# Loading an input on ScalarE's DMA queue instead of SyncE's, with eight half strips of it in SBUF instead of five

## The chip, the cores and the metric

The kernel runs on one core of a Trainium2 chip. Five engines work side by side: TensorE (PE in the profile, its weight loads PEld), VectorE (DVE), ScalarE (ACT), GpSimd (POOL) and SyncE (SP). Each takes its own instructions strictly in order and waits on semaphores for the others. A DMA is issued by an instruction on SP, ACT or POOL. That instruction, too, stands in the engine's order: if it has to wait for a buffer, everything behind it on that engine waits with it. The transfer itself is then run by the core's 16 DMA engines, which all queues share.

The metric is device time in microseconds for one launch, the median of several runs.

## The reference

Two layers on a float32 array `x` of 4 images with 512 channels of 64 x 64 points. Layer 0 is a linear attention with two branches; layer 1 an edge detector with a channel attention and a normalisation over the channels. Cut to what is computed:

```python
# layer 0
qkv = concat(h @ wq.T, h @ wk.T, h @ wv.T)             # 512 -> 3 * 512 channels
pw  = grouped_1x1(depthwise_5x5(qkv))                  # second branch
f   = concat(qkv, pw).reshape(B, 128 heads, 24, N)
query, key, value = relu(f[:, :, :8]), relu(f[:, :, 8:16]), f[:, :, 16:]
scores = einsum('bhdn,bhen->bhde', concat(value, 1), key)
out = einsum('bhde,bhen->bhdn', scores, query)
out = out[:, :, :-1] / (out[:, :, -1:] + 1e-15)
x = batchnorm(conv_1x1(out, proj_kernel)) + x
# layer 1
E  = stack(sobel(x), laplace(x), diagonal(x), gradient(x))   # 3x3 filters per channel
ef = concat_k gelu(batchnorm(w_branch[k] @ E[k]))            # 4 branches of 128 channels
ef = ef * sigmoid(w_att2 @ gelu(w_att1 @ mean(ef)))
z  = w_fuse @ ef
result = gelu(layernorm_over_channels(z)) + x
```

## The kernel before

Everything is float32. An image's 4096 points are cut into eight **strips** of 512; a strip of `x` is [128 partitions, 4 channel blocks, 512]. It is loaded as two **half strips** of two channel blocks each, 512 KB a DMA (`load_x`, L260 to L266). Layer 0 runs as sixteen **groups** (class `Group`, L231): four images `b`, and for each the four groups `g` of 128 channels. A group has two phases, each a list of steps made by hand:

- `keys_and_values` (L579 ff.): for every strip in the order `KV_ORDER = (1, 0, 2, ..., 7)` a projection to keys (`project`, L268, 4 matmuls of 128x512) and one to values (`values`, L300, 16 matmuls of 128x128). Between them stand steps of the previous group: the convolution of its queries, its correlations, its divisions.
- `queries`: for every strip in the order `Q_ORDER = (6, 7, 5, ..., 0)` a projection to queries, with the convolution of the keys, the transposes and the first half of the correlations between them.

`project` ends with copies on ACT: `strip` (L283), for queries also `rq` (L281). The strip then goes out by a POOL DMA (L288) and comes back rolled by row (L295).

**Where x stands.** Image 0 loads all its strips once; twelve of its sixteen half strips have a pool of their own (`x_first`), which is closed after group 3. All later images load each strip anew in every phase, except that the last two strips of one phase are kept for the first two of the next (L277, L309). Their half strips are tiles of the pool `xst` with five buffers. A sixth half strip cannot be loaded before one of the five has had its last matmul. This makes 16 loads for image 0 and 100 for each later image, 316 in all. All are issued on SP (L265), which issues nearly all other loads and stores too: `near` (values for the correlations, L318 out and L458 back), `heads` and `cheads` (L405, L575 out, L659, L661 back), `win` (L708), `ef` (L908), `yr` (L890), `out` (L898), `xr` (L674, x once more, for the residual, in a pool of its own) and the weights.

**The stages behind.** While the groups of image b + 1 run, three generators for image b are advanced between the steps of the groups (`run`, `advance`): `project_out` (1x1 convolution, 8 matmuls for each 128 x 512 block), `edge_branches` (filters on DVE and ACT, then branch matmuls) and `fuse_out` (matmuls, normalisation on ACT, DVE and POOL). How far they are advanced is set by shares of time written into the code (`SHARE_Y`, `WAIT_Y`, ...). The last image's stages run alone, after the last group.

**What sets the order.** For PE the order is the program's own (`manual_schedule` with PE, L108). The other engines' orders, DMA issues included, are made when the kernel is built, by a planner that places an instruction where its inputs and its buffer come free by its own reckoning, and prefers what stands earlier in the program. The order is then fixed. Each DMA issued on SP or ACT also takes one of eight counting semaphores in turn, and waits until the DMA that had it before has landed.

Matmul results go to eight PSUM banks: four for single tiles (`ps`), four for sets of four (`quad`). On SBUF, the pools of the groups end at 156,672 bytes of a partition, and the pools of the stages behind begin at 171,872 at the lowest while the groups run. A half strip takes 4,096.

Of the kernel before, what the change touches and what calls it, by code (L numbers as in the profile page):

```python
# [89 lines left out]
def conv_seq_kernel(  # L90
    ctx: ExitStack, tc, x, wqkv, dpk, wtab, proj, projc, pwk, bn0, consts, vec, watt1, batt1, watt2, wbr, wfuse, out
):
    nc = tc.nc
# [5 lines left out]

    front = ctx.enter_context(ExitStack())  # L100
    keep = front.enter_context(tc.tile_pool(name="keep", bufs=1))
    xst = front.enter_context(tc.tile_pool(name="xst", bufs=5))
    mini = front.enter_context(tc.tile_pool(name="mini", bufs=2))
    gw = front.enter_context(tc.tile_pool(name="gw", bufs=2))
    vals = front.enter_context(tc.tile_pool(name="vals", bufs=VALS))
# [125 lines left out]
    class Group:  # L231
# [28 lines left out]
        def load_x(self, j):  # L260
            xs[self.b, j] = []
            for n in range(2):
                pool = x_first if self.b == 0 and j not in Q_ORDER[:2] else xst
                xt = pool.tile([P, 2, 512], F32, name="xt", tag="xt")
                nc.sync.dma_start(out=xt, in_=x[self.b, j, :, 2 * n : 2 * n + 2, :])  # L265
                xs[self.b, j] += [xt[:, 0, :], xt[:, 1, :]]  # L266

        def project(self, t, j):  # L268
# [873 lines left out]
```

## Time and profile before

| | |
|---|---|
| median of 3 runs | 4831.98 us (4826.22 to 4835.85) |
| profiled execution | 4830.43 us, of which the span from first to last instruction is 4828.6 us |
| mean granted clock of TensorE | 0.968 |
| mean DMA rate | 207 GB/s, 998.02 MB in all |
| PE idle | 4828.6 - 4524.3 = 304.3 us |
| loads of x | 316, from 1.2 to 4038.5 us; the 300 of the later images begin at 94.1 us |

The busy time of each engine by stretch of the span, us:

| stretch, us | what runs | PE | DVE | ACT | POOL | DMA share |
|---|---|---|---|---|---|---|
| 0 to 600 | groups of image 0 | 571.04 | 149.06 | 113.25 | 119.65 | 0.68 |
| 600 to 1100 | image 1, projection out of image 0 | 485.89 | 94.52 | 56.68 | 75.23 | 0.76 |
| 1100 to 2000 | images 1 and 2, edges and fusion of image 0 | 847.89 | 473.96 | 389.04 | 203.02 | 0.77 |
| 2000 to 2450 | image 2, projection out of image 1 | 418.10 | 113.71 | 63.46 | 69.77 | 0.73 |
| 2450 to 3300 | images 2 and 3, edges and fusion of image 1 | 785.45 | 438.84 | 353.39 | 194.69 | 0.77 |
| 3300 to 4040 | image 3, projection out and edges of image 2 | 717.47 | 318.66 | 231.90 | 126.78 | 0.75 |
| 4040 to 4828.6 | rest, no load of x by `load_x` | 698.48 | 518.94 | 380.98 | 198.52 | 0.55 |

A line in a view of waits reads: the engine and line that waited, what ended the wait, then the sum in us, the number of times and the longest. `SPq` is SP's queue of DMA issues; its waits cost nothing by themselves, only through what stands behind them. In a timeline, a line gives the start in us, the length in us, the engine, line, operation and tiles, and in brackets the idle time before it and what ended it.

### The profile page before, as it was taken

The page shows a single profiled execution, that of the slowest core. Times are in us where ns is not written, and L with a number is a line of the kernel's source. Part 1 is how long each engine was busy: PE and PEld are TensorE (multiplying, and loading weights), DVE is VectorE, ACT ScalarE, POOL GpSimd, SP SyncE. Part 2 cuts the span into 40 slices and gives each one's busy share as a digit, 9 for nine tenths or more (in the row PEclk, how much of TensorE's full clock was granted, in tenths as well). Part 3 has the DMA queues.
Part 4 walks back from the last instruction along what each step waited for, and adds up shares of the span by engine and source line. Part 5 has one row for each costly group of instructions (what it writes and reads, how often), then busy time and mean ns, then how long its engine had stood idle before and what let it go on. Part 6 is the DMA issues. An engine that isn't in the chain of part 4 may idle for free. (4 is left out here: it accounts for less than half of the span.)

```text
span 4828.6 us, 86405 instructions
## 1 busy us (share of the span) xinstructions
PE 4524.3 (94%) x35900; PEld 2461.5 (51%) x35900; DVE 2107.7 (44%) x2788; ACT 1588.7 (33%) x2719; POOL 987.7 (20%) x1291
## 2 busy tenths in 40 slices
PE   8999999998999999989899999988999999799987
PEld 5554554444566554444465655444446565344433
DVE  1222222114666634311356663441116666447966
ACT  2122121002554523300245452430014545214765
POOL 2111111111121224311111121431111211111443
PEclk9999999999999999999999999999999999899998
DMA  8666679667787877777678778758668887665445
GB/s 228 186 182 183 184 239 259 176 168 192 231 240 230 260 227 220 227 198 188 175 226 255 227 250 231 226 176 223 177 184 233 243 227 227 184 168 151 155 138 172
DMA packets 498327, 998.02 MB, mean 207 GB/s; under 512 B 189160, under 2 KB 221960, under 8 KB 479504
## 3 DMA queue, kind: packets, MB, share of 16 engines
q1 hardware_dynamic: 415760, 722.43, 50.6%
q0 software_dynamic: 82176, 270.07, 20.3%
q8 instruction: 283, 4.64, 0.4%
q14 instruction: 108, 0.88, 0.1%
HBM read 710.67 MB, written 281.61 MB: 206 GB/s over the span
## 5 line engine op out<-in xcount | busy, mean ns | idle before, releaser
L274 PE MATMUL proj<-xt,w_sb 128*128 128x512 f32 x2048 | 953.0, 608 | 50.3 <-DMA xt<-in_x 28.1
L677 PE MATMUL yps<-hd,fold_sb 128*128 128x512 f32 x2048 | 910.5, 600 | 35.8 <-DMA hd<-heads 27.8
L677 PEld LDWEIGHTS yps<-hd,fold_sb 128*128 128x128 f32 x2048 | 386.4, 192 | 531.7 <-issue 466.0
L274 PEld LDWEIGHTS proj<-xt,w_sb 128*128 128x128 f32 x2048 | 380.7, 194 | 541.7 <-issue 453.9
L418 PE MATMUL cv<-rolled,mat 64*32 64x504 f32 (+2 forms) x10240 | 576.4, 598 | 33.1 <-DMA rolled<-flat 19.1
L866 PE MATMUL zps<-ef,wf_sb 128*128 128x512 f32 (+1 forms) x1056 | 469.1, 597 | 45.6 <-DMA ef<-ef 16.7
L305 PEld LDWEIGHTS val<-w_sb,xt 128*128 128x128 f32 x4096 | 472.6, 193 | 43.4 <-issue 29.9
L305 PE MATMUL val<-w_sb,xt 128*128 128x128 f32 x4096 | 487.9, 278 | 2.4 <-DVE vt L312 1.9
L754 PE MATMUL br<-maps,wbr_sb 128*128 128x256 f32 (+1 forms) x1792 | 463.6, 412 | 0.0
L682 DVE SCALAR_TENSOR_TENSOR yt<-yps,shift,xr 128x512 f32<-128x512 f32 x128 | 95.7, 749 | 804.7 <-PE yps L677 757.8
L754 PEld LDWEIGHTS br<-maps,wbr_sb 128*128 128x128 f32 x1792 | 334.8, 189 | 137.4 <-issue 96.4
L288 POOL DMA_DIRECT2D flat<-strip x256 | 144.9, 566 | 1211.9 <-ACT strip L283 1184.8
L418 PEld LDWEIGHTS cv<-rolled,mat 64*32 64x32 f32 x10240 | 196.7, 109 | 381.9 <-issue 355.3
L295 POOL DMA_DIRECT2D rolled<-flat x512 | 273.3, 538 | 558.2 <-PE cv L418 519.5
L283 ACT COPY strip<-proj 128x512 f32<-128x512 f32 x256 | 149.0, 582 | 671.3 <-PE proj L274 671.3
L473 PE MATMUL corr<-near,ckt 128*32 128x160 f32 x8192 | 336.3, 318 | 26.4 <-DMA near<-near 26.2
L866 PEld LDWEIGHTS zps<-ef,wf_sb 128*128 128x128 f32 x1056 | 203.5, 196 | 293.8 <-issue 221.6
L473 PEld LDWEIGHTS corr<-near,ckt 128*32 128x32 f32 x8192 | 261.1, 112 | 122.0 <-issue 68.2
L686 POOL DMA_DIRECT2D y<-yt x128 | 114.4, 894 | 917.1 <-DVE yt L682 756.2
L730 DVE TENSOR_TENSOR maps<-dv 128x1054 f32<-128x1054 f32 (+1 forms) x112 | 159.8, 1427 | 256.8 <-PE br L754 256.7
L897 POOL TENSOR_TENSOR z<-z,yr 128x512 f32<-128x512 f32 (+1 forms) x132 | 175.5, 1348 | 272.7 <-ACT z L894 150.1
L333 ACT ACTIVATE kt<-tr 128x512 f32<-128x512 f32 x128 | 76.2, 595 | 466.4 <-PE tr L331 466.4
(131 smaller groups left out, 4466.0 us busy)
## 6 DMA issues: line engine op xcount, KB each, us to landing
xt<-in_x SPq DMA_DIRECT2D x316, 512.0 KB
near<-near SPq DMA_DIRECT2D x512, 264.0 KB
rolled<-flat POOLq DMA_DIRECT2D x512, 256.0 KB, 7.4
flat<-strip POOLq DMA_DIRECT2D x256, 256.0 KB, 5.8
win<-y SPq DMA_DIRECT2D x96, 396.0 KB
near<-vt SPq DMA_DIRECT2D x512, 66.0 KB
y<-yt POOLq DMA_DIRECT2D x128, 264.0 KB, 6.3
heads<-q SPq DMA_DIRECT2D x128, 256.0 KB
```

The lines of the kernel that those rows point to most:

```text
L274: nc.tensor.matmul(ps, lhsT=self.w[t][:, c, :], rhs=xs[self.b, j][c], start=(c == 0), stop=(c == NCH - 1))
L283: nc.scalar.copy(s, ps)
L288: nc.gpsimd.dma_start(out=self.flat[t][r, :, b : b + 8, :], in_=rows(s))
L295: nc.gpsimd.dma_start(out=self.rolled[t, half][r::8, :, :], in_=self.flat[t][r % 4, :, at : at + 8, :].rearrange("(n c) b w -> c n (b w)", ...
L305: nc.tensor.matmul(ps[:, ts(c, P)], lhsT=xs[self.b, j][n][:, ts(c, P)], rhs=self.w[VALUE][:, n, :], start=(n == 0), stop=(n == NCH - 1),)
L418: nc.tensor.matmul(rows(banks[2 * s + i])[32 * j : 32 * j + 32, :, c0:c1], lhsT=self.mat[t][q, 4 * s + j, (dx + 2) * 4 : (dx + 2) * 4 + 4, :],
L473: nc.tensor.matmul(self.banks[jj][32 * i : 32 * i + 32, 160 * b : 160 * b + 160], lhsT=self.held["c", i][:, at : at + 32], rhs=v[:, 4 * n ...
L677: nc.tensor.matmul(ps, lhsT=fold_sb[g // NG][:, g % NG, ts(c, P)], rhs=hd[g], start=(g == 0), stop=(g == 2 * NG - 1),)
L730: nc.vector.tensor_sub(flat[:, half : 3 * half - 2], dvs[:, 2 : 2 * half], dvs[:, 0 : 2 * half - 2])
L754: nc.tensor.matmul(rows(ps), lhsT=wbr_sb[:, k, c, :], rhs=rows(maps[:, slot[k], c % 2, :], WB)[:, :, 0:W], start=(c == 0), stop=(c == NCH ...
L866: nc.tensor.matmul(ps, lhsT=wf_sb[:, k, ts(c, P)], rhs=ef[k], start=(k == 0), stop=(k == 3))
L897: nc.gpsimd.tensor_add(rows(z), rows(z), rows(yr, WB)[:, :, 1 : W + 1])
```

## The change

Two lines. The pool `xst` gets eight buffers for five, which takes 3 x 4,096 = 12,288 bytes more of a partition. And the load in `load_x` is issued on ACT (`nc.scalar`) for every image but the first (`self.b` is the image's number); image 0 stays on SP.

```diff
-    xst = front.enter_context(tc.tile_pool(name="xst", bufs=5))
+    xst = front.enter_context(tc.tile_pool(name="xst", bufs=8))
...
-                nc.sync.dma_start(out=xt, in_=x[self.b, j, :, 2 * n : 2 * n + 2, :])
+                (nc.scalar if self.b else nc.sync).dma_start(out=xt, in_=x[self.b, j, :, 2 * n : 2 * n + 2, :])
```

So 300 of the 316 issues move from SP's stream into ACT's, among the evictions of PSUM and the activations. The number of loads, their size and the matmuls that read them stay the same, and so does PE's order. The planner lays out the orders of SP, ACT, DVE and POOL anew.

## The prediction

> **What bounds the kernel now.** I read the page first: engine shares and the span in slices.
>
> ```profile
> span 4828.6 us, 86405 instructions
> ...
> PE 4524.3 (94%) x35900; PEld 2461.5 (51%) x35900; DVE 2107.7 (44%) x2788; ACT 1588.7 (33%) x2719; POOL 987.7 (20%) x1291
> ...
> ACT  2122121002554523300245452430014545214765
> ```
>
> PE sets the time: 94% busy, its order fixed. A change that removes no matmul can only touch the 304.3 us in which PE idles (and the clock it is granted after a pause). ACT is busy a third of the time and below 60% in every slice before the last few. The chain that ended last covers only the final 4.2 us, so the question goes to the waits. Those of PE from 94 to 4039 us, the time in which the moved loads are issued:
>
> ```profile
> PE corr L473 <- DMA near<-near: 24.1, 10, 4.8
> PE proj L274 <- DMA xt<-in_x: 22.8, 3, 21.1
> ...
> PE cden L565 <- ACT strip L283: 14.8, 2, 9.8
> PE yps L677 <- DMA hd<-heads: 13.4, 3, 10.5
> PE ctr L445 <- ACT co L431: 11.8, 4, 4.8
> ```
>
> The reader is to see that x costs PE 22.8 us there, nearly all in one wait, and that ACT's lateness costs it too: all lines of this view ended by ACT add up to 44.7 us. Then SP's own waits over the span:
>
> ```profile
> SPq L265 <- PE proj L274: 270.9, 91, 16.3
> SPq L265 <- PE val L305: 225.3, 45, 25.6
> ...
> SPq L458 <- DMA xt<-in_x: 38.4, 33, 3.0
> ```
>
> SP stood 496.2 us before loads of x whose buffer was still being read. That is the wait which the change carries to ACT. The third line shows the other kind: a load of `near` that waits for a load of x to land, because the two share a counting semaphore. Last, the one long wait, in the timelines of SP and PE:
>
> ```profile
> 3228.37 0.33 SPq L265 DMA_DIRECT2D xt<-in_x  x1
> ...
> 3243.57 0.38 SPq L265 DMA_DIRECT2D xt<-in_x  x1
> ...
> 3261.10 0.91 SPq L644 DMA_DIRECT2D fold_sb<-folded  x2
> 3262.05 2.91 SPq L659 DMA_DIRECT2D hd<-heads  x4
> 3265.00 5.49 SPq L661 DMA_DIRECT2D hd<-cheads  x4
> 3270.71 3.97 SPq L318 DMA_DIRECT2D near<-vt  x4
> 3274.86 0.47 SPq L265 DMA_DIRECT2D xt<-in_x  x1
> ```
>
> ```profile
> 3257.47 1.98 PE L274 MATMUL proj<-xt,w_sb 128*128 128x512 f32 x4
> 3280.57 3.70 PE L274 MATMUL proj<-xt,w_sb 128*128 128x512 f32 x4 [21.12 <-DMA xt<-in_x]
> ```
>
> PE has the first half strip and lacks the second, which stands on SP behind the opening burst of `project_out`.
>
> **The change, part by part.**
>
> *Eight buffers, and SP's burst no longer ahead of x.* With three more buffers a load can go when the one three before it went. The load issued at 3274.86 comes third after one at 3122.86 (the same timeline, earlier), so it can go some 120 us sooner, long before the burst. The wait should vanish, and the two short ones with it: 22.8 us. The four pieces after the wait took 3.70 us where the same four took 1.98 before it, since the granted clock averaged 0.82 from 3226 to 3284: 1.7 us more. Together -24.5; the other end is 0, if the load is placed late on ACT for another reason. I take the whole, since two independent causes of the wait are removed at once.
>
> *300 issues on ACT.* No DMA issue on ACT is in the trace. Low end: SP's shortest, 0.327 us, 98 us in all. High end: POOL's for `y`, 0.894 us, 268 us. I take SP's own sum for these 300, 142.0 us, since both engines only start a transfer there. ACT is busy 1207.7 us up to 4040 and idle for 2832, mostly waiting for PE, so this lies in idle time. What gets through I take from ACT's present share: 44.7 us of PE's waits for 1207.7 us of work, 3.7%, so +5.3 us (3.6 to 9.9). Were the cover gone, all 142 would show.
>
> *The waits of these loads, now on ACT.* Behind a waiting load stand evictions of PSUM (`strip`, `rq`, `kt`, `co`), for which PE waits when its four banks of a kind are full, and the edge activations, for which DVE waits. I set each of the 300 issues of the trace beside the next instruction that ACT has after it in the program's order. In 50 cases the issue ended after that instruction had started, 121.0 us in all, the longest 10.1. Only 4.8 us of this is a buffer still being read: the matmuls that free a half strip also release ACT's next work, so ACT would have stood there anyway. 63.2 us (17 cases) is an earlier DMA that had not landed, and the rest is SP busy with its other entries, which ACT does not inherit. So 68.0 us of hold. Low end 3.7% of it, 2.5 us; high end all. The largest case, four loads around 777 to 787 us, holds ACT some 8 us while PE runs a convolution from 780.6 to 789.2 that asks nothing of ACT; the transposes of `co` at 794.7 would start about 1 us late. One part in eight, then: +8.5 us.
>
> *SP without them.* PE's waits for other transfers of SP come to 63.2 us in that window (near 24.1, ef 16.7, hd 13.4 and 3.9, the attention weights 5.1). The 300 issues are 142.0 of SP's 1237.7 us of issuing there, 11.5%, so -7.3 us. High gain: all 63.2. Loss: x now runs beside those transfers instead of behind or ahead of them; 512 KB at the 214 GB/s of that window are 2.4 us, and for 19 such waits that is +46. I stay near zero, since before the longest of them (hd at 2079.8, ef at 3183.8) no load of x stood directly in SP's queue.
>
> The Trainium skill speaks against more here (DMA: Bandwidth & Descriptors, Rules for kernel authors): spreading DMAs over SP, ACT and GpSimd gives no bandwidth, as all run on the same 16 engines; only issue time is saved. By the rule alone the queue term would be those few us and the 24.5 would have to come from the buffers; by the row, where x sat behind the fourteen issues of a burst, order counts as well. The same page (Anatomy of one DMA) puts every semaphore wait on the issuing sequencer, as the waits of SP above show; by that rule alone up to the 68 us would stand on ACT.
>
> *The sum*, against the profiled execution's 4830.4 us, which is 1.6 below the median: 4830.4 - 24.5 + 5.3 + 8.5 - 7.3 = 4812.4, **some 4813 us**. Its own range is 4800 to 4822.
>
> **The rivals.**
>
> *ACT becomes the late engine: slower.* Place: the query phases, where a projection's eviction follows every 3.6 us, and the edge stages, where ACT and DVE hand tiles back and forth. If the new order leaves all 121 us of the lateness counted above on ACT, four tenths of it reaching PE give 4830.4 - 24.5 - 7.3 + 5.3 + 48 = 4852. It decides from 26.5 us on (22%). For it: 44.7 us of PE's waits already end on ACT, and each pause is followed by matmuls at half clock. Against it: the 4.8 us above, and ACT idle two thirds of the time.
>
> *The wait moves on: no change.* The burst at 3261 still has to land, at a DMA share of 0.82 and 249 GB/s; freed of x, PE may wait 20 us later for `hd` or `near` instead, and newly laid out orders of SP and ACT make as many new short waits as they remove. About 4830. For it: 105.1 us of PE's waits in the window end on DMAs, spread over many places. Against it: PE's first use of `hd` after the burst is beyond 3340, and that was no long wait.
>
> *SP was the real trouble: much faster.* Half of the 63.2 us goes: 4830.4 - 24.5 - 31.6 + 13.8 = 4788. Against it: no x directly ahead of the long ones.
>
> **How the numbers follow.** The forecast 0.38, much faster 0.08, no change 0.19, slower on ACT 0.35. A difference under about 0.2%, 9.7 us, could not be told from none. So faster 0.46, within 0.2% 0.19, slower 0.35. The predicted time is that of the forecast. The range takes in no change and most of the slower case, and leaves out the deep ends: 4795 to 4870.
>
> **What would show it.** Right: PE's wait for xt near 3280 is gone, ACT's rows show issues at L265 of 0.3 to 0.5 us, and PE's waits that end on ACT before 4040 grow by less than 15 us. Wrong: issues on ACT near 0.9 us or ACT waiting long on L265 for landings; `strip`, `co` or `ckt` as new first lines of PE's waits; or a wait of the same size on `hd`, `near` or `ef`. The prediction fails as a whole if the newly laid out orders move more than the terms counted here.

## The result and the profile after

The changed kernel took **4882.55 us** (median of 4 runs, 4878.59 to 4892.26) beside 4832.64 us before (4826.22 to 4835.85): a ratio of 1.0108, 95% interval [1.0089, 1.0126]. It is slower by some 50 us, and the time lies above the predicted range. The page first: the span, the shares of the engines, and of the DMA queues SP's (q1) and ACT's (q10), with packets, megabytes and the share of 16 engines' span.

```profile
span 4882.7 us, 86318 instructions
...
PE 4530.8 (93%) x35900; PEld 2465.1 (50%) x35900; DVE 2107.7 (43%) x2788; ACT 1588.5 (33%) x2721; POOL 986.0 (20%) x1291
...
q1 hardware_dynamic: 372560, 565.12, 39.0%
...
q10 hardware_dynamic: 43200, 157.31, 10.7%
```

PE has 6.5 us more of work than before and 47.6 us more of idling. The work of the other engines is the same, and so is that of the DMA engines: all queues together had 71.4% of 4828.6 us before, 3448 us, and have 70.3% of 4882.7 us now, 3433 us. The mean rate fell from 207 to 204 GB/s only because the span grew. So the DMA engines have no more to do than before: something that PE needs comes later. PE's waits from 94 us to 4085 us, just behind the last load of `x` (before: 94 to 4039 us):

```profile
PE corr L473 <- DMA near<-near: 37.1, 9, 13.2
PE cv L418 <- DMA rolled<-flat: 35.0, 6, 9.0
PE over L396 <- DVE rec L381: 19.5, 12, 6.0
...
PE corr L473 <- DMA near<-vt: 16.2, 1, 16.2
...
PE yps L677 <- DMA hd<-cheads: 13.6, 6, 8.8
```

The wait for `xt` is gone from this window altogether. In its place stand `near` (24.1 us before, 53.3 with both its lines), `rolled` (19.1 before) and `rec` (9.8 before). Summed by what ended them, PE's waits there went from 105.1 to 143.6 us for DMAs, from 53.1 to 59.3 for DVE, and from 44.7 to 45.8 for ACT. The loads themselves, and three of ACT's own waits that a DMA ended, of which there was almost nothing before (22.2 us in this window):

```profile
L265 ACTq DMA_DIRECT2D xt<-in_x x300: 334/334/1427, 25.8 to 4082.1; - x150
L265 ACTq EVENT_SEMAPHORE  x198: 17/17/13817, 605.6 to 4078.7; - x198
```

```profile
ACT kt L333 <- DMA xr<-in_x: 45.2, 1, 45.2
ACT kt L333 <- DMA heads<-q: 15.8, 2, 14.9
...
ACT kt L333 <- DMA near<-vt: 11.1, 1, 11.1
```

In the first block the numbers behind the colon are the shortest, the median and the longest in ns: an issue on ACT costs 334 ns. `kt` uses no data of `xr`, `heads` or `near`. It stands behind a load of `x`, and that load waits for a landing of one of SP's DMAs, because the two took the same counting semaphore in turn: each of the eight carries DMAs of both engines in the trace, 31 to 46 of them ACT's. The longest of the three waits is in good part time in which ACT had nothing to do; how much work was held back is counted below.

How such a hold reaches PE is seen around 3300 us. The timelines of ACT, POOL, SP and PE, after:

```profile
3299.93 0.33 ACTq L265 DMA_DIRECT2D xt<-in_x  x1
3300.30 1.28 ACT L884 ACT_TABLE_LOAD   x1 [8.39 <-DMA near<-vt]
...
3308.64 2.33 POOL L897 TENSOR_TENSOR z<-z,yr 128x512 f32<-128x512 f32 x2 [13.62 <-ACT z L894]
...
3311.40 1.40 SPq L890 DMA_DIRECT2D yr<-y  x2
...
3320.71 2.30 POOL L897 TENSOR_TENSOR z<-z,yr 128x512 f32<-128x512 f32 x2 [8.72 <-DMA yr<-y]
...
3321.92 1.47 SPq L898 DMA_DIRECT2D out<-z  x2
3323.44 0.66 SPq L458 DMA_DIRECT2D near<-near  x1
...
3328.73 3.75 PE L473 MATMUL corr<-near,ckt 128*32 128x160 f32 x64 [13.19 <-DMA near<-near]
```

The input of `rstd` (L884) was there at 3295.7. ACT could not take it, since a load of `x` stood ahead until 3299.9, for the landing of a store `near<-vt`; the load of an activation table (`ACT_TABLE_LOAD`) came only behind it, and `rstd` started at 3301.6. So `z` comes late on POOL; SP stands before `out<-z` and issues the next `yr` and `near` only behind it; and PE waits 13.19 us, for a DMA. The same place in the kernel with eight buffers and `x` on SP (run sp8 below):

```profile
3248.64 0.69 ACT L884 ACTIVATE rstd<-var,ln_eps 128x512 f32<-128x512 f32 x1 [2.55 <-PE var L882]
...
3258.47 1.06 SPq L890 DMA_DIRECT2D yr<-y  x2
...
3264.78 2.31 POOL L897 TENSOR_TENSOR z<-z,yr 128x512 f32<-128x512 f32 x2 [5.73 <-DMA yr<-y]
...
3267.51 0.67 SPq L458 DMA_DIRECT2D near<-near  x1
...
3272.38 4.49 PE L473 MATMUL corr<-near,ckt 128*32 128x160 f32 x64 [3.96 <-DMA near<-near]
```

Here `rstd` follows PE at once, and PE waits 3.96 us. Of the 9.2 us between the two waits, some 6 are the lateness of `rstd`. Some 3 more come with the load of `yr`: from its issue to the start of `z` there are 9.3 us, and here 6.3. A lateness of ACT can thus stand in PE's waits under a DMA's name, and a slower transfer beside it. Over the whole trace I counted how long ACT's next instruction had all its inputs while a load of `x` stood ahead of it: 91 us. That number, called the **hold** below, is worked out from the trace and the program's order. It depends on how the inputs are reckoned: taken from the last of everything that the instruction needs to the end of the load's issue, it is 75 us, and the holds below are 1 to 16 us lower in the same way, in the same order. It does not say how much of it reaches PE; the runs have to.

### The profile page after: what moved, and what is told of

Same layout as the page of the kernel before. It is cut to its first block, busy times and chain, and to the rows that moved or that the text cites. A ratio compares the mean times of both kernels' runs of the same rounds, so it can differ in the third digit from the quotient of the medians.

```text
span 4882.7 us, 86318 instructions
## 1 busy us (share of the span) xinstructions
PE 4530.8 (93%) x35900; PEld 2465.1 (50%) x35900; DVE 2107.7 (43%) x2788; ACT 1588.5 (33%) x2721; POOL 986.0 (20%) x1291
## 5 line engine op out<-in xcount | busy, mean ns | idle before, releaser
L418 PE MATMUL cv<-rolled,mat 64*32 64x504 f32 (+2 forms) x10240 | 578.9, 601 | 53.1 <-DMA rolled<-flat 35.0
```

The lines of the kernel that those rows point to most:

```text
L418: nc.tensor.matmul(rows(banks[2 * s + i])[32 * j : 32 * j + 32, :, c0:c1], lhsT=self.mat[t][q, 4 * s + j, (dx + 2) * 4 : (dx + 2) * 4 + 4, :],
```

## The experiments

Four theories. **A**: the issues on ACT and the waits for landings that tie ACT and SP together (the hold). **B**: the eight buffers. **C**: the orders of the engines that the planner made anew. **D**: the bytes of `x`, which now run in a queue of their own beside SP's chains of stores and loads, where before they stood in one queue with them. Diffs are against the changed kernel. Ratios are to the kernel before, run on the same chip.

### One part of the change at a time

Eight buffers, `x` on SP (sp8):

```diff
-                (nc.scalar if self.b else nc.sync).dma_start(out=xt, in_=x[self.b, j, :, 2 * n : 2 * n + 2, :])
+                nc.sync.dma_start(out=xt, in_=x[self.b, j, :, 2 * n : 2 * n + 2, :])
```

> Eight half strips, all loads of x still issued on SP. Theory A (the queue: ACT is held by loads of x that wait for the landing of SP's DMAs, and SP in turn for x): the loss is gone and the one long wait for x at 3280 us too, so 4805 to 4835 us. Theory B (depth: three more half strips in flight bring x's transfers ahead of near, rolled and hd wherever they are issued): most of the 50 us stays, 4860 to 4885. Theory C (any new layout of the orders of ACT, DVE, SP and POOL costs by chance): anywhere from 4820 to 4880.

4833.07 us, ratio 1.0011 [0.9992, 1.0030]. The queue without the buffers (act5):

```diff
-    xst = front.enter_context(tc.tile_pool(name="xst", bufs=8))
+    xst = front.enter_context(tc.tile_pool(name="xst", bufs=5))
```

> Loads of x of the later images on ACT, five half strips as before. Theory A: the whole loss, 4870 to 4900, and ACT's holds behind loads of x as large as in the changed kernel (some 80 us) or larger, since a buffer comes free later. Theory B: no loss from depth, 4820 to 4845. Theory C: anywhere from 4820 to 4890.

4885.98 us, 1.0131 [1.0098, 1.0164]. The queue makes nearly the whole loss, and B falls. The buffers bring nothing either, though they do take the long wait away. PE's waits of sp8, 94 to 4039 us:

```profile
PE corr L473 <- DMA near<-near: 28.7, 10, 4.1
PE cv L418 <- DMA rolled<-flat: 24.7, 5, 6.7
PE yps L677 <- DMA hd<-heads: 20.3, 4, 10.5
```

No `xt` is left in that window. Set beside before, matmul by matmul, PE gains 21.3 us at the matmul at 3280 us: it had been 7.2 us behind and is 14.0 ahead. At 4039 us it is 10.6 behind, and 4.5 at the end. The gain went in many small waits: these three lines alone are 17.1 us longer.

Image 1 back on SP (act8_from2), and all later images on POOL's queue (pool8):

```diff
-                (nc.scalar if self.b else nc.sync).dma_start(out=xt, ...
+                (nc.scalar if self.b > 1 else nc.sync).dma_start(out=xt, ...
```

```diff
+                (nc.gpsimd if self.b else nc.sync).dma_start(out=xt, ...
```

> As the changed kernel, but image 1's loads of x stay on SP; images 2 and 3 on ACT. The delay of PE against the kernel before, by the traces, was 9 us at the end of image 0 and 27 us by 1150 us, and another 27 us came between 2500 and 4000. Theory A: the part up to 1150 us goes and the rest stays, 4850 to 4865. Theory B: nothing goes, 4870 to 4890. Theory C: anywhere from 4830 to 4890.

> Loads of x of the later images on POOL's queue, which counts on other semaphores than SP and ACT, eight half strips. Theory A: ACT free as before, but strips and rolled strips stand behind x on POOL: if the coupling of SP and ACT is the cause, 4820 to 4860, with ACT's waits that end on DMAs back to some 25 us. Theory B: 4870 to 4900. Theory C: anywhere.

act8_from2: 4868.0 us, 1.0089 [1.0057, 1.0121]: 200 loads on ACT in place of 300, and the loss not clearly smaller. pool8: 4953.35 us, 1.0266 [1.0230, 1.0301]. POOL issues each load in 536 ns, among its own work, and `x` itself is late: PE waited 102.2 us for `xt` over the span. It is slower for another reason, and so tells nothing between A and D.

### The size of the loads

Whole strips (1 MB, four buffers) and quarter strips (256 KB, sixteen buffers), both as many bytes of SBUF as before, on ACT and on SP:

```diff
-            for n in range(2):
...
-                xt = pool.tile([P, 2, 512], F32, name="xt", tag="xt")
-                (nc.scalar if self.b else nc.sync).dma_start(out=xt, in_=x[self.b, j, :, 2 * n : 2 * n + 2, :])
+            xt = pool.tile([P, 4, 512], F32, name="xt", tag="xt")
+            (nc.scalar if self.b else nc.sync).dma_start(out=xt, in_=x[self.b, j, :, :, :])
```

```diff
-            for n in range(2):
+            for n in range(4):
...
-                xt = pool.tile([P, 2, 512], F32, name="xt", tag="xt")
-                (nc.scalar if self.b else nc.sync).dma_start(out=xt, in_=x[self.b, j, :, 2 * n : 2 * n + 2, :])
+                xt = pool.tile([P, 512], F32, name="xt", tag="xt")
+                (nc.scalar if self.b else nc.sync).dma_start(out=xt, in_=x[self.b, j, :, n, :])
```

> x in whole strips of 1 MB, four buffers (the same 64 KB of eight half strips), the later images' 150 loads on ACT. Theory A (each load on ACT takes a counting semaphore in turn with SP's DMAs, so the two queues wait for each other's landings): half as many such waits, so half the loss against the same tiles on SP, some 25 us. Theory D (two queues of transfers running beside each other, by bytes): the difference to the same tiles on SP stays about 50 us.

> Whole strips, four buffers, all loads on SP: the control for the run with whole strips on ACT. Both theories: 4815 to 4850, near the kernel before, since eight half strips on SP cost 0.1%; a whole strip is freed later than its halves, so a little above.

> x in quarter strips of 256 KB, sixteen buffers, the later images' 600 loads on ACT. Theory A: twice as many waits on ACT, a difference of some 100 us to the same tiles on SP, and ACT's waits that end on DMAs well above the 199 us of the changed kernel. Theory D: a difference of about 50 us.

> Quarter strips, sixteen buffers, all on SP: the control for quarter strips on ACT. 316 more issues than with half strips take the eight semaphores in turn on SP alone: 4830 to 4870 by both theories.

On SP the size makes no difference: whole 4817.80 us, 0.9994 [0.9978, 1.0009]; quarters 4826.71 us, 1.0014 [0.9999, 1.0029]. On ACT: whole 4881.92 us, 1.0149 [1.0113, 1.0186]; quarters 4884.60 us, 1.0143 [1.0117, 1.0169]. Half as many issues as in the changed kernel, or twice as many, and holds of 45 and of 196 us, with the loss about the same: theory A in its simple form, so much for each issue, falls. With whole strips the loss against the same tiles on SP, 64 us by the medians, is larger than the hold of 45 us. In the quarters ACT does reach PE more: PE's waits ended by ACT are 92.0 us over the span against 59.2 on SP, which no other of these pairs shows (65.3 after, 64.0 in sp8).

### The orders

The orders of SP, ACT, DVE and POOL, all but the loads of `x` themselves, were forced to those of another kernel: the changed kernel with the orders of sp8 (act8_sp_orders), and sp8 with the orders of the changed kernel (sp8_act_orders). The function is called once at the end of the program; `ORDERS` holds the order of each engine.

```diff
+def keep_orders(nc, tc):
...
+        for a, b in zip(names, names[1:]):
+            tc.add_manual_dep(traced[b], a, info, reason="order")
```

> The changed kernel (loads of x on ACT, eight half strips), with the orders of DVE, POOL, ACT and SP, loads of x apart, held to those of the run with eight half strips on SP. Theory C (the planner's new layout of the orders costs): the loss is gone, 4820 to 4840 us. Theory A or D (loads on ACT cost by themselves, through the semaphores shared with SP or through two queues side by side): 4865 to 4890.

> Eight half strips, all loads of x on SP, with the orders of DVE, POOL, ACT and SP, loads of x apart, held to those of the changed kernel. Theory C: the loss comes with the orders, 4865 to 4890 us. Theory A or D: near the run on SP with its own orders, 4820 to 4845.

4869.30 us, 1.0094 [1.0064, 1.0123], and 4825.23 us, 1.0008 [0.9990, 1.0026]. The loss stays with the queue, whichever orders are kept. C falls.

### Bytes and issues taken apart

Each strip as a quarter and three quarters, one on ACT, one on SP. The large one on ACT is act_3of4; act_1of4 has the two queues exchanged.

```diff
-            for n in range(2):
...
+            for lo, n, name, q in ((0, 1, "x1", nc.sync), (1, 3, "x3", nc.scalar)):
+                xt = pool.tile([P, n, 512], F32, name=name, tag=name)
+                (q if self.b else nc.sync).dma_start(out=xt, in_=x[self.b, j, :, lo : lo + n, :])
```

> Each strip of x (1 MB) is loaded in two DMAs into two tiles: one channel block (256 KB) and three (768 KB), four buffers of each kind, as many bytes of SBUF as the eight half strips. For all images but the first the large DMA is issued on ACT, the small one on SP: 150 issues on each queue, three quarters of the bytes on ACT's. Theory A (ACT and SP hold each other up, since an issue of either waits for the landing of an earlier DMA of the other; the loss goes with the issues on ACT, not with their bytes): the same loss here and in the reversed split, both near that of whole strips on ACT (4882) or both near half of it (4850), within 12 us of each other. Theory D (transfers of x in a ring of their own run beside SP's stores and loads of near and heads, and slow the chains through DRAM; the loss goes with the bytes on ACT's ring): 4860 to 4880 here, against 4830 to 4845 in the reversed split.

> The same two tiles per strip, reversed: the small DMA (256 KB) is issued on ACT, the large one (768 KB) on SP, for all images but the first: again 150 issues on each queue, but a quarter of the bytes on ACT's. Theory A: the time of the other split within 12 us, 4850 to 4885 both, with the waits of ACT that a DMA ends at 80 us or more, as with whole strips on ACT (84.7). Theory D: 4830 to 4845, some 30 us below the other split; PE's waits that a DMA ends 120 to 135 us, against 150 to 165 there.

act_3of4: 4843.64 us, 1.0084 [1.0062, 1.0106]. act_1of4: 4806.98 us, 1.0018 [1.0001, 1.0036] (this chip ran the kernel before in 4802.90). PE's waits of the one and the other:

```profile
PE corr L473 <- DMA near<-near: 34.3, 9, 6.9
PE cv L418 <- DMA rolled<-flat: 28.0, 5, 8.1
...
PE corr L473 <- DMA near<-vt: 11.4, 1, 11.4
```

```profile
PE corr L473 <- DMA near<-near: 31.9, 13, 5.1
PE cv L418 <- DMA rolled<-flat: 20.8, 4, 6.5
```

150 issues on ACT in both, and the loss is 37 us apart by the medians, 32 by the ratios: it goes with the bytes, as D has it. (PE's waits on DMAs, 147.0 and 115.2 us over the span, are each a little below what D expected.) But the hold differs too, 49.6 us against 16.6, so A is not yet held fixed. For that, most of each half strip goes on SP and a small part on ACT, with all 300 issues there. First by partitions (act_sliver, with sp_sliver as control), then along the free dimension (act_eighth, sp_eighth):

```diff
+                nc.sync.dma_start(out=xt[0:120], in_=x[self.b, j, 0:120, 2 * n : 2 * n + 2, :])
+                (nc.scalar if self.b else nc.sync).dma_start(out=xt[120:128], in_=x[self.b, j, 120:128, 2 * n : 2 * n + 2, :])
```

```diff
+                nc.sync.dma_start(out=xt[:, 0:896], in_=src[:, 0:896])
+                (nc.scalar if self.b else nc.sync).dma_start(out=xt[:, 896:1024], in_=src[:, 896:1024])
```

> Eight half strips as in the changed kernel, but of each half strip only the last 8 of its 128 partitions (32 KB) are loaded on ACT for all images but the first, the other 120 (480 KB) on SP: 300 issues on ACT, as many as in the changed kernel and each with its wait for an earlier landing, with 9.8 MB in place of 157.3 on ACT's queue. Theory A (the holds of ACT and SP behind each other's landings cost the time): the loss stays, 0.8 to 1.4% slower than before, with holds on ACT as after (91 us; ACT's waits that a DMA ends 150 us or more). Theory D (the bytes that run beside SP's stores and loads cost it): within 0.3% of the control with both parts on SP, PE's waits that a DMA ends within 15 us of it.

> Control: the same two parts of each half strip, both loaded on SP: 632 issues of x on SP in place of 316. Theory A and D alike: within 0.3% of before (as with quarter strips on SP, which had 600 issues and a ratio of 1.0014), unless the split by partitions makes the loads themselves slower, which would show as waits of PE for xt.

> The split of every half strip again, now along the free dimension so that both parts keep all 128 partitions: 896 of 1024 values a partition (448 KB) on SP, the last 128 (64 KB) on ACT for all images but the first: 300 issues on ACT with their waits, 19.7 MB on its queue. Theory A: the holds of ACT alone cost most of the loss, 0.8 to 1.4% above the control with both parts on SP, with holds of 90 us or more on ACT. Theory D: the loss goes with the bytes, an eighth of 50 us, so within 0.3% of the control. A mixture: 0.3 to 0.7%, as the split by partitions suggests (1.0250 against its control's 1.0197).

> Control: the same two parts, both on SP. With quarter strips (600 issues of x on SP, 1.0014) as the nearest case, both theories expect 4815 to 4845, if the parts of 64 KB, made of 512-byte pieces, transfer in proportion; if they don't, PE waits for xt as with the parts of 8 partitions (28.5 us there).

The split by partitions was slow in itself: 4925.71 us on SP alone, 1.0197 [1.0173, 1.0222], against 4950.95 us and 1.0250 [1.0222, 1.0277]. Against this control the loss is 0.53% (uncertain by some 0.37% either way) with 9.8 MB on ACT, more than D expected and less than A, so it does not decide between them. The second split was not slow in itself: sp_eighth 4827.01 us, 0.9998 [0.9978, 1.0017], and act_eighth 4845.51 us, 1.0020 [1.0003, 1.0038]. ACT's longest waits of act_eighth that a DMA ended:

```profile
ACT co L439 <- DMA xt<-in_x: 37.8, 5, 18.8
ACT kt L335 <- DMA near<-near: 34.5, 1, 34.5
ACT co L439 <- DMA hd<-cheads: 28.0, 1, 28.0
```

ACT is held 117 us here, more than in the changed kernel, and its waits that a DMA ended are 249 us over the span, against 199 there. Yet the kernel loses 0.2% against its control by the ratios (a difference that is uncertain by some 0.26% either way), 18.5 us by the medians. So if a hold costs PE in the changed kernel what it costs here, the holds are real, but they are the smaller part.

The kernels that have `x` on ACT, by megabytes there. Left out are act5 (1.0131) and act8_sp_orders (1.0094), with the same loads as the changed kernel, and act_sliver, which is slow by its split:

| kernel | issues on ACT | MB on ACT's queue | hold, us | ratio to before | the same on SP |
|---|---|---|---|---|---|
| act_eighth | 300 | 19.7 | 117 | 1.0020 | 0.9998 |
| act_1of4 | 150 | 39.3 | 17 | 1.0018 | not run |
| act8_from2 | 200 | 104.9 | 51 | 1.0089 | 1.0011 |
| act_3of4 | 150 | 118.0 | 50 | 1.0084 | not run |
| the changed kernel | 300 | 157.3 | 91 | 1.0108 | 1.0011 |
| act_quarter16 | 600 | 157.3 | 196 | 1.0143 | 1.0014 |
| act_whole4 | 150 | 157.3 | 45 | 1.0149 | 0.9994 |

The ratios broadly follow the third column, not the second or the fourth; those of the last three rows have intervals that overlap. None of the kernels is faster than the kernel before beyond its interval.

Where the time goes can be read from one profiled execution of each, set beside before matmul by matmul. The changed kernel falls back 16.7 us between 600 and 750 us of the trace of before, and 24.8 us between 2500 and 3000; sp8 gains 0.3 and 4.2 us there. act_eighth falls back 2.7 and 13.6 us, and its control gains 0.4 and 6.2. So with an eighth of the bytes the first loss is nearly gone, but not the second, which the bytes alone do not explain.

## Why the prediction was wrong

Two steps failed, the first term of the sum and the last.

**The waits of x, -24.5.** They went, as said, and the matmul at 3280 us no longer waits. (In sp8 its load is issued at 3129.2 us, 145.7 us sooner than before; the prediction said some 120, where its own lines allow 152.) But the step "I take the whole, since two independent causes of the wait are removed at once" argued only that the wait would vanish, not that the time would stay won. sp8 measures the term: +0.11% [-0.08, +0.30], about +5 us. The rival "the wait moves on" was right here. What was held against it was misread: PE's first use of `hd` after the burst is not beyond 3340 us but at 3300.0, though it was no wait.

**300 issues on ACT, +5.3, and their hold, +8.5.** Their sum came out near, partly by luck. An issue takes 334 ns against SP's shortest of 327, and all 300 take 110.0 us where 142.0 had been counted; the hold was 91 us where 68.0 had been counted, and the landings of `near` and `heads`, not buffers, make most of it. act_eighth, with the issues and a hold of 117 us, lost 11 us (by the ratios, 0.22% of 4830) to 18.5 (by the medians) against its control, where the two terms made 13.8. But the path was wrong: the price had been read from PE's waits on ACT, which grew by 1.1 us, and the cost came in part as waits on DMAs, as around 3300 us.

**SP without x, -7.3.** This step failed too, and by more. Its loss end was named, "x now runs beside those transfers instead of behind or ahead of them ... +46", and put aside with "I stay near zero, since before the longest of them ... no load of x stood directly in SP's queue". That reason looked at what stood before the transfers of before; it says nothing of what will run beside them after. Against sp8 the queue costs 1.0108 - 1.0011 = 0.97%, 47 us; less 11 to 18.5 for issues and holds, 28 to 36 us are left to the bytes. That is a remainder and no measurement of its own, and both differences it is made from are uncertain by some 13 us either way.

With +5 for the first term and 47 for all that the queue costs, 4830.4 + 5 + 47 = 4882, beside 4882.55; it must come out, since the last part is what was left over. Either failure alone would have left the time inside the range: 4842 us with the first term at +5, 4848 to 4856 with the last at +28 to +36. The range ended at 4870, and both came together.

**The rival of a late ACT**, 4852, had the right sign and the wrong price: four tenths of the hold were to reach PE, and in act_eighth about a tenth to a sixth did. **What would show it** was met on all three points (no wait at 3280, issues of 0.3 to 0.5 us, ACT's share of PE's waits up by less than 15 us) while the forecast failed. Of the signs against it, two came. ACT did wait at L265 for landings: up to 13.8 us, and its waits that a DMA ended are 199 us over the span, where they were 26.5. And there were new waits on `near`, though smaller than the 21.1 us that went: 13.19 us at the same place, and 16.2 us on `near<-vt` near 722 us.

**How the bytes cost is only partly shown.** A store `near<-vt` of 66 KB took 6.33 us from issue to landing before, as a mean from 650 to 4039 us, 6.39 in sp8, and 7.66 after: 8.19 with a load of `x` in flight beside it, 5.23 without (before: 6.58 and 5.44). The loads `near<-near` did not lengthen: 9.1 us, and 9.2 before. The store lengthens with the bytes on ACT: 6.34 in act_eighth, 6.38 in act_1of4, 6.83 in act_3of4. SP then waits longer for these stores ahead of the loads of `near`, over the span:

```profile
SPq L458 <- DMA near<-vt: 95.4, 40, 5.7
```

in place of 68.8 us before and 62.5 in sp8. But the store does not settle it. With whole strips on SP it took 6.86 us, and nothing was lost (0.9994). With quarter strips on ACT it took 6.50 us (6.06 on SP), and the loss was as large as ever; there the holds of 196 us may have had more of it, as the 33 us more in PE's waits on ACT suggest. So how the bytes cost PE its time stays open, and the share of each in the other sizes stays an estimate. A kernel in which ACT's loads wait for no landing of SP's, which would give the bytes alone, was not tried.

The Trainium skill (DMA: Bandwidth & Descriptors, Queues, rings and completion order) says that a DMA engine takes turns, packet by packet, between the queues that have work for it. That fits stores which take longer while `x` runs in the other queue; no trace here shows the turns themselves. The rule that spreading over queues gives no bandwidth (Rules for kernel authors) held: the DMA engines' total time hardly changed (3448 us before, 3433 after). That it only saves issue time leaves out what was lost here.

## What to carry to other kernels

A wait that vanishes is worth only what the next wait leaves of it; undo one half of a change and time the other before the gain is booked. Moving large loads to a second queue is not free: here it cost 1%, and more with more bytes there. It takes them out of one order, lets them run beside the small stores on which a store-and-load chain through DRAM depends, and ties two engines together through the landings that each waits for. To learn which of the two costs, change the bytes on the queue with the issues fixed and the issues with the bytes fixed; and look behind a wait on a DMA for an engine that was late before the DMA was issued.

## What the hardware showed beyond that

A wait instruction of its own stands ahead of 198 of the 300 loads on ACT. Half of them took 17 ns, the longest 13.8 us; act_eighth has 210 of them, up to 16.4 us, and lost 0.2% against its control. Splitting a half strip into 120 and 8 partitions lost 2% with both parts on SP: PE waited for `x` again, 28.5 us over the span where sp_eighth has 5.2, and the queue's share rose from 50.6% to 52.5% for the same 722.43 MB. What else the 2% is made of was not traced. The wait of sp_sliver from 94 to 4085 us:

```profile
PE proj L275 <- DMA xt<-in_x: 18.8, 6, 7.6
```

A split of the same tile along the free dimension, into 448 and 64 KB, cost nothing (0.9998). The Trainium skill (DMA: Bandwidth & Descriptors, Why a DMA increments its semaphore by 16 and not by 1) states that the engines which a DMA uses are the largest number up to 16 that divides the size of its slowest dimension, here the partitions, by which 8 partitions would go to 8 engines; the slower loads agree with it. No view here counts the engines, but the trace of sp_sliver has 9 updates of a semaphore by the DMA for each of the 316 loads of 8 partitions, and 16 for each load of 128.
